# Where a scan gets its first state: from a pointer to the last one, or folded into the first column of its input

## The chip, the cores and the metric

The kernel runs on one core of one Trainium2 chip. The metric is the device time of one execution in microseconds, as the median of several runs. The profile is one execution, recorded by the hardware profiler.

## What is computed

The input x is (4, 128, 128, 128) in float32. Layer 0 is a Mamba block over each image as a sequence of 16384 positions; layer 1 is a spectral layer (Fourier transforms, a filter mix, a residual). What matters here is the recurrence of layer 0, with 256 inner channels and 16 states per channel:

```python
A = -jnp.exp(A_log)
def step(h, inp):
    d_t, B_t, C_t, u_t = inp
    dA = jnp.exp(d_t[:, :, None] * A)
    h = h * dA + d_t[:, :, None] * B_t[:, None, :] * u_t[:, :, None]
    y = jnp.einsum('bds,bs->bd', h, C_t)
    return (h, y)
```

Before it come four matrix products, a convolution of four taps, a softplus (delta) and a SiLU (u); behind it the gate, the output product and the norms.

## The kernel before

**Tiling.** A chunk is 512 positions of one image; there are 32 chunks per image and 128 in all, k from 0 to 127. The 256 channels are two halves (j). A tile has 128 partitions, which are 32 channels by 4 of the 16 states. A half needs 16 such tiles per chunk. They are worked in units of four, so a chunk has 8 units (two halves by four rounds r) of four places (p = 0 to 3), and a unit is two pairs of places. One pair is one slot: slots 0, 2, 4, ... of a chunk hold places 0 and 1 of a unit, slots 1, 3, 5, ... hold places 2 and 3. `place(r, p)` rotates which of the four channel groups m a place holds.

**One place of a unit.** ACT computes da = exp(delta * A), 512 wide (`exps`, L400), into PSUM for places 1 to 3 and into SBUF for place 0. The product du*B is `b`: for places 1 to 3 POOL multiplies tiles in SBUF into `hb` (`dbu`, L370), for place 0 PE builds it in PSUM by a transpose (`dbu_turn`, L390). DVE scans along the 512 positions (L419), the state being state * da + b. The scan takes its first state from `st`, a column with the last state of the same place in the chunk before; where a chunk opens an image, the first state is the constant 0. Then h is multiplied by C into `hb`: on DVE (L421) where `by_vector` says so, which is places 2 and 3 with a few exceptions, else on POOL (L426), where places 0 and 1 are mostly one instruction of 1024. ACT copies the last state into `st` (L422, L427). PE sums over states and channels (`sums`, L440), with `gate` (L450) behind it.

**Where the large tiles come from.** rdu and rdelta hold du and delta of one half, repeated over the states. ACT makes delta in slot 6 (`dt_act`), POOL makes du (`du_pool`, L319) in slot 7, SP stores both to DRAM (dd), and SP loads them back four times over, a load for each 32 partitions (`rep_load`, L327): for j = 0 in slot 9, for j = 1 in slot 16. The slots here are those of the chunk before: what chunk k needs at its first slot is made while chunk k-1 is scanned. rB and rC come the same way.

**The order.** It is written out by hand. Each step is put into a slot and a phase, and `manual_schedule` issues slot after slot, in each slot phase after phase:

```python
for phase in ("turn", "sums", "pe", "exps", "late", "act", "pool", "dbu", "early", "gate", "scans", "dve", "end"):
    for f in todo[n, phase]:
        f()
```

Each engine has one queue, which runs in this order. POOL's is dbu(u+1), product(u), dbu(u+2), product(u+1), and so on, with `du_pool` once a chunk. A dbu is one instruction of 1536 elements for rounds 0 and 1 and two (512 and 1024) for rounds 2 and 3, since `place` wraps round there.

**Buffers.** hb has four, h three, rdu and rdelta two each, da one in PSUM for each of places 1 to 3. The small tiles of the pool `tiny` have two. `spectrum`, which transforms some channels of layer 1 early, beside the scans, has its own tiles fx, fs and fq.

Of the kernel before, what the change touches and what calls it, by code (L numbers as in the profile page):

```python
# [26 lines left out]
F32 = mybir.dt.float32  # L27
AF = mybir.ActivationFunctionType
ALU = mybir.AluOpType
# [4 lines left out]
P = 128  # L34
T = 512
# [11 lines left out]
def kernel(ctx: ExitStack, tc: tile.TileContext, a: dict, out: bass.AP):  # L47
# [106 lines left out]
    spec = [dpool.tile([H, C, 2, WF], F32, tag=f"spec_{b}", name=f"spec_{b}") for b in range(EARLY)]  # L154
    shared = SimpleNamespace(**{k: v for k, v in locals().items() if k not in ("ctx", "tc")})
    block0(tc, shared)
    block1(tc, shared)


def block0(tc, s):  # L160
    nc, B, NCH, NH, NS, NG, ND, R, NX, KC, HALO, C, L, NF, DI = (
        s.nc, s.B, s.NCH, s.NH, s.NS, s.NG, s.ND, s.R, s.NX, s.KC, s.HALO, s.C, s.L, s.NF, s.DI,
    )
    NT, TH, HP = T // P, T // 2, P // 2
    with ExitStack() as ctx:
        def pool(name, bufs, **kw):
            return ctx.enter_context(tc.tile_pool(name=name, bufs=bufs, **kw))

        p1 = pool("p1", 1)
        p2 = pool("p2", 2)  # L170
        hpool = pool("hb", 4)
        tiny = pool("tiny", 2)
# [13 lines left out]
        st = {}  # L186
        stats, outs = s.stats, s.outs

        def pre(k):
# [3 lines left out]
            b, i = divmod(k, NCH)  # L193
            d = st[k] = {}
# [127 lines left out]
            def rep_load(j):  # L322
# [9 lines left out]
                (NP - 2, "pe", z_mm), (NP - 1, "act", z_act), (NP + 2, "act", z_silu), (3, "pe", xd_mm), (4, "act", xd_act), (5, "pe", dt_mm), (5, "pe", xd_turn),  # L332
                (5 if k else 7, "act", bc_load), (6, "act", dt_act), (7, "act", xd_turn_act), (7, "pool", du_pool),
                (8, "pe", partial(du_turn, 0)), (9, "act", partial(rep_load, 0)),
                (8, "pool", partial(bt_act, 0, 0, 1)), (9, "act", partial(bt_act, 0, 1, 5)),
                (10, "act", partial(bt_act, 0, 5, 8)), (11, "pe", partial(du_turn, 1)),
                (11, "pool", partial(bt_act, 1, 0, 1)), (12, "act", partial(bt_act, 1, 1, 2)),
# [7 lines left out]
        def norming(k):  # L345

            return k >= NCH and 2 <= k % NCH < 2 + NCH // 2

        def place(r, p):


            return (p - r) % ND

        def by_vector(k, j, r, p):

            if norming(k):
                return p > 1 and (k % 2 == 1 or (j, r, p) != (1, 2, 2))
            return p > 1 or (k % 2 == 1 and (j, r, p) == (1, 2, 1))

        def dbu(u):  # L360

            k, r = divmod(u, NH * NG)
            j, r = divmod(r, NG)
            d = st[k]
            hb = d["hb", j, r] = hpool.tile([P, ND, T], F32, tag="hb", name=f"hb_{k}_{j}_{r}")
            p = 1
            while p < NG:
                m = place(r, p)
                n = min(NG - p, ND - m)
                nc.gpsimd.tensor_tensor(  # L370
                    hb[:, p : p + n, :], d["du", j][:, m : m + n, :], d["B"][:, p - 1 : p - 1 + n, :], ALU.mult
                )
                p += n

        def pair(n):

            k, r = divmod(n, NP)
            u, p = divmod(r, ND // 2)
            j, r = divmod(u, NG)
            return k, j, r, 2 * p  # L380

        def dbu_turn(n):

            k, j, r, p = pair(n)
            d = st[k]
            if p == 0:
                b = d["b0"] = psd.tile([P, T], F32, tag="b0", name=f"b0_{k}_{j}_{r}")
                for t in range(NT):
                    src = d["bt"][:, t, j * ND + place(r, 0), :, :].rearrange("p s d -> p (s d)")
                    nc.tensor.transpose(b[:, t * P : (t + 1) * P], src, s.ident)  # L390

        def exps(n, qs):

            k, j, r, p = pair(n)
            d = st[k]
            for q in qs:
                m = place(r, p + q)
                c = (j * NG + p + q) * ND + m
                da = (psd if p + q else p2).tile([P, T], F32, tag=f"da{p + q}", name=f"da{p + q}_{k}_{j}_{r}")
                nc.scalar.activation(da, d["delta", j][:, m, :], AF.Exp, scale=s.amat[:, c : c + 1])  # L400
                d["da", j, r, p + q] = da

        def scans(n):


            k, j, r, p = pair(n)
            d = st[k]
            hb = d["hb", j, r]
            das = [d.pop(("da", j, r, p + q)) for q in range(2)]
            dve = [q for q in range(2) if by_vector(k, j, r, p + q)]  # L410
            pool = [q for q in range(2) if q not in dve]
            last = d["last", j, r, p] = tiny.tile([P, 2], F32, tag=f"st{j}_{r}_{p}", name=f"st_{k}_{j}_{r}_{p}")
            if pool:
                h = p2.tile([P, 2, T], F32, tag="h", name=f"h_{k}_{j}_{r}_{p}", bufs=3)
            for q in range(2):
                b = hb[:, p + q, :] if p + q else d.pop("b0")
                init = 0.0 if k % NCH == 0 else st[k - 1]["last", j, r, p][:, q : q + 1]
                o = das[q] if q in dve else h[:, q, :]
                nc.vector.tensor_tensor_scan(o, das[q], b, init, ALU.mult, ALU.add)  # L419
            for q in dve:  # L420
                nc.vector.tensor_tensor(hb[:, p + q, :], das[q], d["C"][:, p + q, :], ALU.mult)  # L421
                nc.scalar.copy(last[:, q : q + 1], das[q][:, T - 1 : T])  # L422
            if pool:
                q = slice(pool[0], pool[-1] + 1)
                ps = slice(p + pool[0], p + pool[-1] + 1)
                nc.gpsimd.tensor_tensor(hb[:, ps, :], h[:, q, :], d["C"][:, ps, :], ALU.mult)  # L426
                todo[n + 1, "late"].append(partial(nc.scalar.copy, last[:, q], h[:, q, T - 1]))  # L427

        def sums(u):

# [44 lines left out]
        def spectrum(b, c0, n):  # L475

            g = {}

            def load():
                g["x"] = p1.tile([s.H, 3, s.W], F32, tag="fx", name=f"fx_{b}_{c0}")  # L480
                nc.sync.dma_start(out=g["x"][:, 0:n], in_=s.x1[b][c0 : c0 + n].rearrange("c h w -> h c w"))

            def over_h():
                g["pa"] = psp.tile([s.W, 3, 2 * s.WF], F32, tag="pp", name=f"pp_fa_{b}_{c0}")
                for q in range(n):
                    nc.tensor.matmul(g["pa"][:, q], g["x"][:, q], s.fh, start=True, stop=True)

            def evict():
                g["sa"] = p1.tile([s.W, 3, 2 * s.WF], F32, tag="fs", name=f"fs_{b}_{c0}")
                nc.scalar.copy(g["sa"][:, 0:n], g["pa"][:, 0:n])  # L490

            def over_w():
                half = s.H // 2
                g["px"] = psp.tile([s.H, 3, 2 * s.WF], F32, tag="pp", name=f"pp_fx_{b}_{c0}")
                for q in range(n):
                    re, im = g["sa"][:, q, 0 : s.WF], g["sa"][:, q, s.WF :]
                    for (data, a, b_), start in (((re, s.fwr, s.fwr), True), ((im, s.fwi, s.fwm), False)):
                        for at, w in ((0, a), (1, b_)):
                            o = g["px"][at * half : (at + 1) * half, q]
                            nc.tensor.matmul(o, data[:, at : at + half], w, start=start, stop=not start)  # L500

            def store():
                x = p1.tile([s.H, 3, 2, s.WF], F32, tag="fq", name=f"fq_{b}_{c0}")
                nc.scalar.copy(x[:, 0:n].rearrange("h c r k -> h c (r k)"), g["px"][:, 0:n])  # L504
                nc.sync.dma_start(out=s.spec[b][:, c0 : c0 + n], in_=x[:, 0:n])

            return [
                (4, "pe", load), (12, "pe", over_h), (12, "end", evict), (13, "pe", over_w), (13, "end", store),
            ]

        n_chunks = B * NCH
        todo = defaultdict(list)
# [33 lines left out]
        for n in range(n_chunks * NP):  # L546
            if n % 2 == 0:
                todo[n - 3, "early"].append(partial(exps, n, (0,)))
            todo[n - 1, "exps"].append(partial(exps, n, (1,) if n % 2 == 0 else (0, 1)))
            todo[n - 1, "turn"].append(partial(dbu_turn, n))  # L550
            todo[n, "scans"].append(partial(scans, n))
            if n % 2 == 0:
                todo[n - 2, "dbu"].append(partial(dbu, n // 2))
            else:
                todo[n + 2, "sums"].append(partial(sums, n // 2))
        slots = [n for n, _ in todo]
        with tc.manual_schedule():
            for n in range(min(slots), max(slots) + 1):
                for phase in ("turn", "sums", "pe", "exps", "late", "act", "pool", "dbu", "early", "gate", "scans", "dve", "end"):
                    for f in todo[n, phase]:  # L560
                        f()

# [509 lines left out]
```

## Time and profile before

| what | value |
|---|---|
| median of 3 runs | 7097.85 us (7094.02 to 7100.94) |
| profiled execution, its own time | 7100.83 us |
| its span, first to last instruction | 7099.1 us |
| busy DVE, POOL, ACT, PE | 96%, 96%, 87%, 80% of the span |
| scans, L419 | 4096 instructions, 60 to 6384 us |
| of these from the constant 0 | 128 |
| last stage (layer 1) | 6384 us to the end |

Busy shares are of the whole span, and the two stages have different limits. A line of a group tells its line in the code, the engine, the operation and its tiles (out<-in), then how often it ran, its busy time in us and the mean of one in ns, and behind the last bar the time that the engine stood idle before it and what ended that. Consecutive DVE instructions overlap by some tens of ns, so the sum of means is above the busy time; the distance of starts is what one costs. A DMA's row tells its issue; its landing is told apart.

### The profile page before, as it was taken

What the parts mean: (1) busy time and instruction counts of PE and PEld (TensorE: products, weight loads), DVE (VectorE), ACT (ScalarE), POOL (GpSimd) and SP (SyncE); (2) the same over time, 40 slices, a digit from 0 to 9 for tenths busy, and PEclk for the clock granted to TensorE, in tenths of its full rate; (3) what the DMA queues carried; (4) which work ended last, traced back from release to release, by engine and by line L of the source; (5) the groups of instructions that cost most, each with busy time, mean ns of one, the idle gap of its engine ahead of it and who ended that gap; (6) DMA issues with size and microseconds to landing.
All of it is one profiled execution on the core that took longest, in us unless ns stands there. A gap on an engine that the chain in (4) does not pass through costs nothing.

```text
span 7099.1 us, 95554 instructions
## 1 busy us (share of the span) xinstructions
PE 5656.9 (80%) x28724; PEld 2700.3 (38%) x28724; DVE 6843.7 (96%) x7901; ACT 6144.4 (87%) x13836; POOL 6807.6 (96%) x3010
## 2 busy tenths in 40 slices
PE   6777777787777778787787778887778787877999
PEld 2333333333333333333333333333333333327888
DVE  6999999999999999999999999999999999997877
ACT  6888888888888888888989888898988989878886
POOL 6999999999999999999999999999999999997887
PEclk8988898888989989999999999999999999989999
DMA  6667667667787767777777777777878777768865
GB/s 141 160 153 164 159 149 165 160 150 175 179 196 181 188 169 167 181 181 179 192 193 196 189 174 177 174 184 172 200 188 200 191 170 178 169 143 293 273 218 190
DMA packets 759513, 1288.54 MB, mean 182 GB/s; under 512 B 81728, under 2 KB 192848, under 8 KB 758992
## 3 DMA queue, kind: packets, MB, share of 16 engines
q1 hardware_dynamic: 758848, 1282.16, 72.5%
q8 instruction: 226, 3.70, 0.2%
q14 instruction: 295, 2.42, 0.1%
q10 hardware_dynamic: 144, 0.26, 0.0%
HBM read 1025.52 MB, written 256.58 MB: 181 GB/s over the span
## 4 chain that ended last, share of the span: by engine, by line
ACT 30%; DVE 24%; POOL 18%; PE 10%; issue 10%; DMA 7%; SPq 1%; DVEq 0%; ACTq 0%; POOLq 0%
DVE da L419 12%; ACT da L400 12%; POOL hb L370 10%; POOL hb L426 7%; DVE h L419 7%; ACT L400 3%; DVE hb L421 3%; DMA rdelta<-dd 2%; ACT bt L313 2%; PE px L892 2%; DMA rdu<-dd 2%; ACT L247 2%; ACT L283 1%; ACT delta L283 1%; PE y L440 1%
## 5 line engine op out<-in xcount | busy, mean ns | idle before, releaser
L370 POOL TENSOR_TENSOR hb<-rdu,rB 128x1536 f32<-128x1536 f32 (+2 forms) x1536 | 3612.4, 2370 | 41.6 <-DMA rdelta<-dd 21.2
L400 ACT ACTIVATE da<-rdelta,amat 128x512 f32<-128x512 f32 x4096 | 2792.3, 699 | 123.3 <-DVE h L419 119.3
L426 POOL TENSOR_TENSOR hb<-h,rC 128x1024 f32<-128x1024 f32 (+1 forms) x1048 | 2411.1, 2302 | 89.3 <-DVE h L419 76.6
L419 DVE TENSOR_TENSOR_SCAN da<-da,st,hb 128x512 f32<-128x512 f32 x2000 | 2449.3, 1268 | 38.0 <-ACT da L400 27.1
L421 DVE TENSOR_TENSOR hb<-da,rC 128x512 f32<-128x512 f32 x2064 | 1309.7, 673 | 2.2
L419 DVE TENSOR_TENSOR_SCAN h<-da,st,b 128x512 f32<-128x512 f32 x992 | 1258.7, 1269 | 1.9 <-PE b L390 1.9
L440 PE MATMUL y<-hb,sel 128*32 128x512 f32 x8192 | 1243.4, 681 | 2.9 <-POOL hb L426 2.7
L419 DVE TENSOR_TENSOR_SCAN h<-da,st,hb 128x512 f32<-128x512 f32 x976 | 1223.1, 1255 | 1.4 <-ACT da L400 1.4
L390 PE MATMUL b<-ident,bt 128*128 128x128 f32 x4096 | 723.7, 298 | 448.9 <-DVE h L419 325.2
L239 PE MATMUL pp_cv<-xm,wck 128*128 128x512 f32 x2048 | 1013.7, 640 | 1.5 <-ACT xm L222 0.8
L313 ACT ACTIVATE bt<-pt_dut,xdt 128x256 f32<-128x256 f32 x2048 | 837.6, 473 | 181.1 <-PE pt_dut L302 180.9
L390 PEld LDWEIGHTS b<-ident,bt 128*128 128x128 f32 x4096 | 524.6, 151 | 943.2 <-DVE h L419 650.7
L422 ACT COPY st<-da 128x1 f32<-128x1 f32 x2064 | 267.9, 160 | 441.3 <-DVE hb L421 437.0
L239 PEld LDWEIGHTS pp_cv<-xm,wck 128*128 128x128 f32 x2048 | 396.0, 204 | 651.7 <-issue 420.8
L302 PE MATMUL pt_dut<-ident,du 128*128 128x128 f32 x1024 | 207.8, 337 | 407.2 <-POOL du L319 391.4
L850 POOL TENSOR_TENSOR wb<-wb,term 128x1040 f32<-128x1040 f32 x166 | 398.8, 2403 | 62.0 <-ACT term L840 56.6
L436 PE MATMUL y<-u,diag 128*128 128x512 f32 x512 | 303.3, 676 | 183.7 <-DVE zs L450 181.8
L277 PE MATMUL pp_dt<-xd,wdt 128*128 128x256 f32 x1024 | 299.2, 418 | 149.9 <-ACT pp_o L464 141.2
L302 PEld LDWEIGHTS pt_dut<-ident,du 128*128 128x128 f32 x1024 | 132.2, 165 | 652.6 <-POOL du L319 528.5
L400 ACT ACT_TABLE_LOAD x262 | 336.1, 1283 | 12.2 <-DMA rdelta<-dd 7.6
L319 POOL TENSOR_TENSOR du<-delta,u 128x1024 f32<-128x1024 f32 x128 | 301.1, 2353 | 29.4 <-ACT delta L283 27.9
L228 PE MATMUL pp_z<-xm,win 128*128 128x512 f32 x512 | 275.6, 636 | 59.5 <-ACT fq L504 53.7
(167 smaller groups left out, 8209.6 us busy)
## 6 DMA issues: line engine op xcount, KB each, us to landing
rdelta<-dd SPq DMA_DIRECT2D x1024, 256.0 KB, 4.8
rdu<-dd SPq DMA_DIRECT2D x1024, 256.0 KB, 7.8
rC<-bc SPq DMA_DIRECT2D x512, 256.0 KB, 7.4
rB<-bc SPq DMA_DIRECT2D x512, 192.0 KB, 4.6
dd<-delta SPq DMA_DIRECT2D x256, 256.0 KB, 7.7
dd<-du SPq DMA_DIRECT2D x128, 512.0 KB, 6.6
ft<-in_filt_w SPq DMA_DIRECT2D x108, 520.0 KB, 6.7
ob<-o SPq DMA_DIRECT2D x128, 256.0 KB, 2.1
```

What stands on the lines that cost most here:

```text
L239: nc.tensor.matmul(ps["cv", j], w, d["xm"][:, t : t + T], start=t == 0, stop=t == KC - 1)
L302: nc.tensor.transpose(ps["dut"][:, 2 * t + j, :], d["du"][:, j, at : at + P], s.ident)
L313: nc.scalar.activation(d["bt"][:, 2 * h + t, :, q, :], src, AF.Copy, scale=d["xdt"][:, 2 * h + t, R + q : R + q + 1])
L370: nc.gpsimd.tensor_tensor(hb[:, p : p + n, :], d["du", j][:, m : m + n, :], d["B"][:, p - 1 : p - 1 + n, :], ALU.mult)
L390: nc.tensor.transpose(b[:, t * P : (t + 1) * P], src, s.ident)
L400: nc.scalar.activation(da, d["delta", j][:, m, :], AF.Exp, scale=s.amat[:, c : c + 1])
L419: nc.vector.tensor_tensor_scan(o, das[q], b, init, ALU.mult, ALU.add)
L421: nc.vector.tensor_tensor(hb[:, p + q, :], das[q], d["C"][:, p + q, :], ALU.mult)
L426: nc.gpsimd.tensor_tensor(hb[:, ps, :], h[:, q, :], d["C"][:, ps, :], ALU.mult)
L436: nc.tensor.matmul(y, s.diag[:, j, :], d["u"][:, j, :], start=True, stop=False)
L440: nc.tensor.matmul(y[m * DG : (m + 1) * DG, :], s.sel, d["hb", j, r][:, p, :], start=False, stop=r == NG - 1)
L850: nc.gpsimd.tensor_tensor(wb, wb, u[n].terms[f], ALU.add)
```

## The change

The scans of places 1 to 3 start from the constant 0 in every chunk. What the first state would have added at the first position, da[0] * last state, is added to the first column of b instead, so the states are the same. For this:

- POOL's dbu writes columns 1 to 511 of `hb` alone.
- `first_products` (DVE): for one half, the first column of du*B for all three places and four channel groups, 12 elements per partition, read from column 0 of rdu and rB; and, unless the chunk opens an image, the exponents delta[0] * A, 16 elements, from column 0 of rdelta. `first_exp` (ACT) takes the exponential, `first_mult` (DVE) multiplies by the last states, `first_add` (DVE) adds both, twice over, into a tile of 24 (a copy where the chunk opens an image).
- `first` (ACT), once per unit, in a new phase ahead of "early": a copy of three of these elements into column 0 of places 1 to 3 of `hb`.
- The last states of a half become one tile of 16 columns; the order of the places in it lets one product take them all. Place 0 still reads its first state from there.
- `by_vector` gives DVE the product of place 1 in (j, r) = (1, 2) in all chunks without `norming`, where it was every second; and in chunks with it, POOL's exception (1, 2, 2) goes.
- `spectrum` works in one tile instead of three.

```diff
+                (12, "dve", partial(first_products, k, 0)), (13, "late", partial(first_exp, k, 0)),
+                (14, "gate", partial(first_mult, k, 0)), (14, "dve", partial(first_add, k, 0)),
+                (20, "dve", partial(first_products, k, 1)), (21, "late", partial(first_exp, k, 1)),
+                (21, "dve", partial(first_mult, k, 1)), (22, "gate", partial(first_add, k, 1)),
...
             if norming(k):
-                return p > 1 and (k % 2 == 1 or (j, r, p) != (1, 2, 2))
-            return p > 1 or (k % 2 == 1 and (j, r, p) == (1, 2, 1))
+                return p > 1
+            return p > 1 or (j, r, p) == (1, 2, 1)
...
-                    hb[:, p : p + n, :], d["du", j][:, m : m + n, :], d["B"][:, p - 1 : p - 1 + n, :], ALU.mult
+                    hb[:, p : p + n, 1:],
+                    d["du", j][:, m : m + n, 1:],
+                    d["B"][:, p - 1 : p - 1 + n, 1:],
+                    ALU.mult,
...
+        def first_products(k, j):
+            d = st[k]
+            du = d["du", j][:, :, 0:1].rearrange("p m o -> p o m")
+            b = d["B"][:, :, 0:1]
+            f = d["f", j] = tiny.tile([P, NG - 1, 1, ND], F32, tag=f"f{j}", name=f"f_{k}_{j}")
+            shape = [P, NG - 1, ND]
+            nc.vector.tensor_tensor(f[:, :, 0, :], du.to_broadcast(shape), b.to_broadcast(shape), ALU.mult)
+            if k % NCH:
+                e = d["e", j] = tiny.tile([P, NG, ND], F32, tag=f"e{j}", name=f"e_{k}_{j}")
+                a = s.amat.rearrange("p (j g m) -> p j g m", j=NH, m=ND)[:, j]
+                now = d["delta", j][:, :, 0:1].rearrange("p m o -> p o m")
+                nc.vector.tensor_tensor(e, a, now.to_broadcast([P, NG, ND]), ALU.mult)
+
+        def first_exp(k, j):
+            if k % NCH:
+                nc.scalar.activation(st[k]["e", j], st[k]["e", j], AF.Exp)
+
+        def first_mult(k, j):
+            if k % NCH:
+                e = st[k]["e", j]
+                nc.vector.tensor_tensor(e, e, st[k - 1]["last", j], ALU.mult)
+
+        def first_add(k, j):
+            shape = [P, NG - 1, 2, ND]
+            f = st[k]["f2", j] = tiny.tile(shape, F32, tag=f"g{j}", name=f"g_{k}_{j}")
+            b = st[k]["f", j].to_broadcast(shape)
+            if k % NCH:
+                e = st[k]["e", j][:, 1:].rearrange("p g (c m) -> p g c m", c=1)
+                nc.vector.tensor_tensor(f, b, e.to_broadcast(shape), ALU.add)
+            else:
+                nc.vector.tensor_copy(f, b)
+
+        def first(u):
+            k, r = divmod(u, NH * NG)
+            j, r = divmod(r, NG)
+            at, step = ND - r + 1, 2 * ND + 1
+            f = st[k]["f2", j].rearrange("p g c m -> p (g c m)")
+            nc.scalar.copy(st[k]["hb", j, r][:, 1:NG, 0], f[:, at : at + 2 * step + 1 : step])
...
-                init = 0.0 if k % NCH == 0 else st[k - 1]["last", j, r, p][:, q : q + 1]
+                m = place(r, 0)
+                init = 0.0 if p + q or k % NCH == 0 else st[k - 1]["last", j][:, 0, m : m + 1]
...
-                g["x"] = p1.tile([s.H, 3, s.W], F32, tag="fx", name=f"fx_{b}_{c0}")
+                g["f"] = p1.tile([s.H, 3, 2 * s.WF], F32, tag="fx", name=f"fx_{b}_{c0}")
...
                 todo[n - 2, "dbu"].append(partial(dbu, n // 2))
+                todo[n - 1, "first"].append(partial(first, n // 2))
```

More of the change, by code (lines that the diff above doesn't have):

```diff
@@ L411, in scans @@
             pool = [q for q in range(2) if q not in dve]
-            last = d["last", j, r, p] = tiny.tile([P, 2], F32, tag=f"st{j}_{r}_{p}", name=f"st_{k}_{j}_{r}_{p}")
+            if (j, r, p) == (j, 0, 0):
+                d["last", j] = tiny.tile([P, NG, ND], F32, tag=f"st{j}", name=f"st_{k}_{j}")
+            last = d["last", j].rearrange("p g m -> p (g m)")
+            at = [(p + q) * ND + place(r, p + q) for q in range(2)]
             if pool:
@@ L421, in scans @@
                 nc.vector.tensor_tensor(hb[:, p + q, :], das[q], d["C"][:, p + q, :], ALU.mult)
-                nc.scalar.copy(last[:, q : q + 1], das[q][:, T - 1 : T])
+                nc.scalar.copy(last[:, at[q] : at[q] + 1], das[q][:, T - 1 : T])
             if pool:
@@ L426, in scans @@
                 nc.gpsimd.tensor_tensor(hb[:, ps, :], h[:, q, :], d["C"][:, ps, :], ALU.mult)
-                todo[n + 1, "late"].append(partial(nc.scalar.copy, last[:, q], h[:, q, T - 1]))
+                a, b = at[pool[0]], at[pool[-1]]
+                to = last[:, a : b + 1 : max(b - a, 1)]
+                todo[n + 1, "late"].append(partial(nc.scalar.copy, to, h[:, q, T - 1]))
         def sums(u):
@@ L479, in load @@
             def load():
-                g["x"] = p1.tile([s.H, 3, s.W], F32, tag="fx", name=f"fx_{b}_{c0}")
-                nc.sync.dma_start(out=g["x"][:, 0:n], in_=s.x1[b][c0 : c0 + n].rearrange("c h w -> h c w"))
+                g["f"] = p1.tile([s.H, 3, 2 * s.WF], F32, tag="fx", name=f"fx_{b}_{c0}")
+                nc.sync.dma_start(out=g["f"][:, 0:n, 0 : s.W], in_=s.x1[b][c0 : c0 + n].rearrange("c h w -> h c w"))
             def over_h():
@@ L485, in over_h @@
                 for q in range(n):
-                    nc.tensor.matmul(g["pa"][:, q], g["x"][:, q], s.fh, start=True, stop=True)
+                    nc.tensor.matmul(g["pa"][:, q], g["f"][:, q, 0 : s.W], s.fh, start=True, stop=True)
             def evict():
-                g["sa"] = p1.tile([s.W, 3, 2 * s.WF], F32, tag="fs", name=f"fs_{b}_{c0}")
-                nc.scalar.copy(g["sa"][:, 0:n], g["pa"][:, 0:n])
+                nc.scalar.copy(g["f"][:, 0:n], g["pa"][:, 0:n])
             def over_w():
@@ L495, in over_w @@
                 for q in range(n):
-                    re, im = g["sa"][:, q, 0 : s.WF], g["sa"][:, q, s.WF :]
+                    re, im = g["f"][:, q, 0 : s.WF], g["f"][:, q, s.WF :]
                     for (data, a, b_), start in (((re, s.fwr, s.fwr), True), ((im, s.fwi, s.fwm), False)):
@@ L502, in store @@
             def store():
-                x = p1.tile([s.H, 3, 2, s.WF], F32, tag="fq", name=f"fq_{b}_{c0}")
-                nc.scalar.copy(x[:, 0:n].rearrange("h c r k -> h c (r k)"), g["px"][:, 0:n])
+                nc.scalar.copy(g["f"][:, 0:n], g["px"][:, 0:n])
+                x = g["f"].rearrange("h c (r k) -> h c r k", r=2)
                 nc.sync.dma_start(out=s.spec[b][:, c0 : c0 + n], in_=x[:, 0:n])
@@ L558, in block0 @@
             for n in range(min(slots), max(slots) + 1):
-                for phase in ("turn", "sums", "pe", "exps", "late", "act", "pool", "dbu", "early", "gate", "scans", "dve", "end"):
+                for phase in ("turn", "sums", "pe", "exps", "late", "act", "pool", "dbu", "first", "early", "gate", "scans", "dve", "end"):
                     for f in todo[n, phase]:
```

## The prediction

> **What bounds the kernel now.** I read busy time by engine, then the stages, then the groups by form, then the timeline of one chunk. In a middle stage (columns: PE, PEld, DVE, ACT, POOL busy):
>
> ```profile
> DVE  6999999999999999999999999999999999997877
> POOL 6999999999999999999999999999999999997887
> 3300.00:4840.00 1540.00, 1227.57 (x5834) 534.63 (x5834) 1525.84 (x1627) 1381.44 (x3149) 1515.56 (x662) 0.94 0.76 184
> ```
>
> DVE works 99% of these 1540 us, POOL 98%, ACT 90%. The scans (60 to 6384 us) are one stage in which DVE and POOL are both full: a microsecond gained on one alone is lost to the other soon, and a microsecond in which DVE stands still is not made good. What a first state costs stands in the groups by form (count | busy, mean ns), since the first chunk of each of the 4 images already starts from 0:
>
> ```profile
> L419 DVE TENSOR_TENSOR_SCAN da<-da,st,hb 128x512 f32<-128x512 f32 x2000 | 2449.3, 1268 | 38.0 <-ACT da L400 27.1 <-POOL hb L370 8.9 <-issue 1.2
> L419 DVE TENSOR_TENSOR_SCAN h<-da,st,hb 128x512 f32<-128x512 f32 x976 | 1223.1, 1255 | 1.4 <-ACT da L400 1.4
> L419 DVE TENSOR_TENSOR_SCAN da<-da,hb 128x512 f32<-128x512 f32 x64 | 74.5, 1210 | 1.1 <-issue 0.9
> L419 DVE TENSOR_TENSOR_SCAN h<-da,hb 128x512 f32<-128x512 f32 x32 | 38.3, 1197 | 3.9 <-POOL hb L370 3.7 <-ACT da L400 0.2
> ```
>
> So a constant saves 58 ns. Starts agree: a unit (4 scans, 2 products) takes 5.89 us in the timeline (1019.46 to 1025.35) and 5.65 us in the first chunk (59.91 to 65.56).
>
> Two things in the timeline decide. First, how DVE fares beside POOL when it has small operands in SBUF:
>
> ```profile
> 90.05 3.44 POOL L370 TENSOR_TENSOR hb<-rdu,rB 128x1536 f32<-128x1536 f32 x1
> 90.92 2.65 DVE L138 TENSOR_SCALAR weff<-wagg,gn_gamma 128x128 f32<-128x128 f32 x1
> 93.44 2.36 POOL L426 TENSOR_TENSOR hb<-h,rC 128x1024 f32<-128x1024 f32 x1
> 93.61 2.34 DVE L139 SCALAR_TENSOR_TENSOR weff<-wagg,gn_gamma,weff 128x128 f32<-128x128 f32 x1
> 95.87 0.15 DVE L144 TENSOR_TENSOR bias<-pp_bias,agg_b 128x1 f32<-128x1 f32 x1
> ```
>
> L138 ends 0.08 us after POOL's product, L139 at 95.95 when the next ends (95.80); L129, the like of L138 with POOL idle, took 0.23 us. L144 has one input in PSUM and doesn't wait. Nor does any scan, product or gate: each has one input in PSUM. Second, when rdu of the next chunk lands:
>
> ```profile
> 1018.64 2.35 POOL L319 TENSOR_TENSOR du<-delta,u 128x1024 f32<-128x1024 f32 x1
> ...
> 1021.01 0.37 SPq L320 DMA_DIRECT2D dd<-du  x1
> ...
> 1027.39 1.74 SPq L327 DMA_DIRECT2D rdu<-dd  x4
> ...
> 1033.04 1.26 DVE L419 TENSOR_TENSOR_SCAN da<-da,st,hb 128x512 f32<-128x512 f32 x1
> ...
> 1034.33 0.69 DVE L421 TENSOR_TENSOR hb<-da,rC 128x512 f32<-128x512 f32 x1
> ...
> 1037.32 3.42 POOL L370 TENSOR_TENSOR hb<-rdu,rB 128x1536 f32<-128x1536 f32 x1
> DMA to landing us min/median/max: 5.4/7.8/10.5
> ```
>
> The scan at 1033.04 is the second of slot 12, L421 its product; DVE leaves the slot at 1034.94. The last rdu load (from 1028.69) lands 7.8 us later, at 1036.46. Over the 46 chunks whose four landings the trace tells, the last landing is 1.3 to 6.0 us, 3.1 in the mean, after the end of that scan. POOL's first product of rdu starts 3.9 us after it (median), so today almost nobody waits.
>
> **What the Trainium skill says.** SBUF — State Buffer, section "Who interferes with whom": a DVE instruction with two SBUF inputs, or in a two-port mode, and a GpSimd instruction reading SBUF exclude each other for the whole instruction; the later one blocks. L138, L139 and L144 agree. Perfetto Trace Analysis, section "Optimizing Scalar/DVE Operations": some 60 ns fixed for DVE on SBUF; the 512-element product starts the next after 0.59 us, which agrees.
>
> **The change, part by part.** Gains and small prices on DVE:
> - 3 scans in 4, 124 chunks of 128: 2976 x 0.058 = 173 us off.
> - by_vector moves a 512 product from POOL to DVE in 40 even chunks without norm and 24 with: 64 x 0.59 = 38 us on. POOL loses 40 x (2.37 - 1.29) + 24 x 1.29 = 74 us.
> - Small instructions: first_products 256 + 248, first_mult 248, first_add 256 = 1008, estimated at 0.08 us of pitch (60 ns and 12 to 24 elements): 81 us.
> Sum -54 us, -0.4 per chunk.
>
> New stalls of DVE, per chunk:
> - **first_products of j=0, behind slot 12, needs rdu.** It comes a product (0.6) later than the scan's end; DVE is 3 x 0.17 = 0.5 us faster over the three units since du, and POOL's du some 0.25 earlier (the product before it starts 0.33 us after slot 6's scans now, at once when POOL waits for them). Wait: 3.1 - 0.6 + 0.5 - 0.25 = 2.75 us. Behind it on DVE's queue stand the second product, slot 13's scans and products; for those wait ACT (first_exp, copies, exps), POOL's next product, PE. Below: 0.95 (smallest landing); above: 5.65.
> - **The port there.** POOL's own next product (1536, 3.4 us) waits for the same landing. Either it gets in before the first small product or between the two, and DVE waits 3.4; or both small ones slip through: 0. I take 3.4, as L138/L139 show POOL getting in between.
> - first_mult in slot 14 finds POOL idle (its next product needs slot 14's scans): 0. first_add behind those scans: 0, as DVE's queue goes on before POOL hears.
> - **The port at j=1.** Behind slot 4 POOL is just done with its dbu (median rest 0.05 us). If the pair of small products passes, POOL runs its product (2.3) and the dbu of unit 4 (3.4) until 5.75 after slot 4; first_mult, behind slot 5 (3.4 later), waits some 2.3, and first_add follows free. If it doesn't pass, the second waits 2.3 there and first_mult is free. 2.3 either way, up to 3.5.
> Sum 2.75 + 3.4 + 2.3 = 8.45; with -0.4, 8.05 us per chunk, x 127 = 1022 us.
>
> Elsewhere, at no cost:
> - ACT gets 1024 `first` copies of 3 elements (0.19, like st<-h) and 248 exps (0.2 to 0.3): some 255 us, 2.0 per chunk; copies of last states +40. It idles some 5 us per chunk in that stage. A scan of place 1 now waits for `first`, which stands behind slot n-1's ACT work: ACT has 4.7 us from the release of da1 to that scan, the exp and copy take 0.9, and `first` is late only where that slot holds over 3.5 us. Stalls give it more room. Without that cover: up to 2 us in one or two units of a chunk.
> - `first` and POOL's dbu write different columns of hb; were they ordered, ACT would wait for a dbu that is done within 2 us of that point.
> - POOL's 511-wide rows: no view shows them. Rows of 65 in the last stage (L917) cost 1394 ns for 520 elements, where the 512 row takes 1283: under 15 ns a row. Bounds -0 to +10% of dbu's 28 us, which POOL then has room for.
> - Spectrum's three tiles become one: the next load waits for a store seven slots (20 us) earlier that lands in 1.9. SP's queue gets no new DMA.
> - `last` as one tile: ACT's copies write other columns; readers come a chunk later.
> - The last stage (6384 to the end) is untouched.
>
> The profiled execution took 7100.83 us around a span of 7099.1, 3 us above the median of 7097.85. 7097.85 + 1022 is about 8120.
>
> **The rivals.**
> - *Port harmless for tiny operands, landing not*: 2.75 - 0.4 = 2.35 per chunk, 298 us: 7395. For it: no small product of two SBUF tensors runs beside POOL today, and 12 elements might pass. Against: L139.
> - *Every small instruction blocked*: three waits for a whole POOL product (2.4) and five for the rest of one (1.3, half the length-weighted mean of POOL's instructions) make 13.7; with POOL busy 0.8 of the time, 11; with the landing 13.35 per chunk, 1695 us: 8793. For it: POOL is full today. Against: it idles once DVE stalls.
> - *Faster*: the landing comes before slot 12 ends and the port isn't contended; then -54 on DVE, -74 on POOL: 7045. It decides if rdu lands 3 us sooner; only an earlier du on POOL would do that. Against: not one of the 46 landings is early enough.
> - That scans don't take a constant is excluded by the code and the 128 that already do.
>
> **How the numbers follow.** Main case 0.5 (7850 to 8400), port harmless 0.2 (7300 to 7500), more blocking 0.22, faster 0.04, other small losses 0.04, of which 0.01 no change. A change under 0.2% couldn't be told from none here. Range 7390 to 8600.
>
> **What would show it.** Right: scans of places 1 to 3 near 1200 ns; DVE idle at the first small product of j=0, ended by a DMA of rdu, some 350 us in all; small products with means of 0.5 us and more, their maximum about 3.4; POOL busy below 90% in this stage and idle before L426's line for DVE; ACT below 90%. Wrong: small products at 0.15 us throughout, no wait for rdu, or a chunk period below 49 us.

## The result, and the profile after

The changed kernel takes 7899.61 us (median of 4 runs, 7887.12 to 7914.8) against 7098.72 us before: a ratio of 1.1131, with a 95% interval of 1.1117 to 1.1145. It is 801 us slower. Its profiled execution spans 7885.3 us, 786 more than the profile before.

The stage that stood at 99% for DVE and 98% for POOL, in the third image of the changed kernel (same columns: PE, PEld, DVE, ACT, POOL busy; at the end the granted TensorE clock, the share of the DMA engines and GB/s):

```profile
3660.00:5400.00 1740.00, 1301.53 (x5779) 558.58 (x5782) 1674.05 (x1869) 1405.03 (x3425) 1485.56 (x647) 0.85 0.67 161
```

A chunk of the last three images takes 56.3 us where it took 49.5; one of the first image takes 53.2 where it took 48.8. DVE is still busy for 96% of the stage, but POOL only for 85%, and ACT for 81%. The granted TensorE clock is lower than before, 0.85 instead of 0.94, but that isn't what costs the time: DVE stands idle for PE for under 3 us in all the scans together. "Busy" has to be read with care here. The prediction's "port" is the way to SBUF that a DVE instruction with two SBUF inputs and POOL can only have one at a time, and an instruction that stands and waits for it counts as busy. The groups by form show it (count | busy, mean ns | idle before, releaser):

```profile
L475 DVE TENSOR_TENSOR_SCAN da<-da,hb 128x512 f32<-128x512 f32 x2128 | 2481.4, 1208 | 10.6 <-ACT hb L442 7.4 <-ACT da L452 1.9 <-issue 0.3
...
L421 DVE TENSOR_TENSOR e<-e,st 128x16 f32<-128x16 f32 x248 | 323.3, 1304 | 0.8 <-ACT e L416 0.8
L412 DVE TENSOR_TENSOR e<-amat,rdelta 128x16 f32<-128x16 f32 x248 | 300.1, 1210 | 0.2
...
L407 DVE TENSOR_TENSOR f<-rdu,rB 128x12 f32<-128x12 f32 x256 | 142.2, 555 | 227.2 <-DMA rdu<-dd 99.5 <-DMA xr<-in_x 62.4 <-DMA rdelta<-dd 40.2
...
L431 DVE TENSOR_TENSOR g<-f,e 128x24 f32<-128x24 f32 x248 | 41.5, 167 | 4.2
```

The scans are at 1208 ns, as the constant promised. But products of 16 elements take as long as scans of 512, in the mean. Of the 227 us of idle time ahead of L407, 40 belong to the first chunk of all. The other 187 are the wait for rdu, though the profile puts 72 of them down to DMAs of x, which L407 does not read: all of them go when L407 no longer reads the rdu that has just been loaded (below, "No landing to wait for"). And POOL, that was full, now waits for DVE (its products with C; they read h, so they wait for the scans, even where the profile names the small instruction that ended last):

```profile
L482 POOL TENSOR_TENSOR hb<-h,rC 128x1024 f32<-128x1024 f32 x944 | 2230.1, 2362 | 966.7 <-DVE g L431 421.6 <-DVE h L475 368.3 <-DVE f L407 92.5
```

The timeline of one chunk has both places. For j = 0, behind slot 12:

```profile
1172.80 3.59 POOL L374 TENSOR_TENSOR hb<-rdu,rB 128x1022 f32<-128x1022 f32 x2
...
1174.30 0.69 DVE L477 TENSOR_TENSOR hb<-da,rC 128x512 f32<-128x512 f32 x1
1175.62 0.80 DVE L407 TENSOR_TENSOR f<-rdu,rB 128x12 f32<-128x12 f32 x1 [0.62 <-DMA rdu<-dd]
1176.35 1.31 DVE L412 TENSOR_TENSOR e<-amat,rdelta 128x16 f32<-128x16 f32 x1
1176.36 1.26 POOL L482 TENSOR_TENSOR hb<-h,rC 128x512 f32<-128x512 f32 x1
```

DVE stands idle for 0.62 us until rdu lands. Then L407 starts at 1175.62 and ends at 1176.42, with POOL's running product (1176.39); L412 ends at 1177.66, with POOL's next (1177.62). For j = 1, behind slots 4 and 5:

```profile
1148.05 0.14 DVE L407 TENSOR_TENSOR f<-rdu,rB 128x12 f32<-128x12 f32 x1
1148.11 0.17 DVE L412 TENSOR_TENSOR e<-amat,rdelta 128x16 f32<-128x16 f32 x1
1148.20 2.37 POOL L482 TENSOR_TENSOR hb<-h,rC 128x1024 f32<-128x1024 f32 x1 [0.24 <-DVE f L407]
...
1150.51 3.45 POOL L374 TENSOR_TENSOR hb<-rdu,rB 128x1533 f32<-128x1533 f32 x1
1151.64 2.36 DVE L421 TENSOR_TENSOR e<-e,st 128x16 f32<-128x16 f32 x1
1154.03 0.18 DVE L431 TENSOR_TENSOR g<-f,e 128x24 f32<-128x24 f32 x1
```

The first two pass before POOL starts; L421 arrives 1.13 us into POOL's product and ends with it (1153.96), and L431 is free again. It is so in the whole trace: the 360 small products that took over 0.3 us all end 0.02 to 0.05 us behind an instruction of POOL, and none of the 640 others lies inside one. The trace's records split by half and line give the bill per chunk (means; own duration about 0.16):

| DVE | j = 0 | j = 1 |
|---|---|---|
| idle ahead of L407, for a DMA | 1.47 | 0 |
| L407, f | 0.96 | 0.15 |
| L412, exponents | 2.25 | 0.17 |
| L421, first_mult | 0.29 | 2.32 |
| L431, first_add | 0.15 | 0.18 |

The stalls are 1.47 + 0.81 + 2.09 + 0.14 + 2.17 = 6.7 us per chunk, 837 us over the chunks that have them. The means hide a spread: the idle time ahead of L407 is 2.72 us where the chunk that is being scanned has `norming` work too (48 of them), 0.94 in the 47 others of the last three images and 0.38 in the first image.

### The profile page after: what moved, and what is told of

It is laid out like the page before. It is cut to its first block, busy times and chain, and to the rows that moved or that the text cites. A ratio compares the mean times of both kernels' runs of the same rounds, so it can differ in the third digit from the quotient of the medians.

```text
span 7885.3 us, 98596 instructions
## 1 busy us (share of the span) xinstructions
PE 5926.0 (75%) x28724; PEld 2785.8 (35%) x28724; DVE 7459.9 (95%) x8973; ACT 6309.2 (80%) x15148; POOL 6740.8 (85%) x2986
## 5 line engine op out<-in xcount | busy, mean ns | idle before, releaser
L374 POOL TENSOR_TENSOR hb<-rdu,rB 128x1533 f32<-128x1533 f32 (+2 forms) x1536 | 3599.1, 2359 | 21.9 <-DMA rdelta<-dd 21.1
L482 POOL TENSOR_TENSOR hb<-h,rC 128x1024 f32<-128x1024 f32 (+1 forms) x1024 | 2332.0, 2277 | 966.7 <-DVE g L431 421.6
L475 DVE TENSOR_TENSOR_SCAN da<-da,hb 128x512 f32<-128x512 f32 x2128 | 2481.4, 1208 | 10.6 <-ACT hb L442 7.4
L397 PE MATMUL b<-ident,bt 128*128 128x128 f32 x4096 | 782.8, 320 | 793.0 <-DVE h L475 755.0
L498 PE MATMUL y<-hb,sel 128*32 128x512 f32 x8192 | 1369.5, 746 | 2.7 <-POOL hb L482 2.6
L475 DVE TENSOR_TENSOR_SCAN h<-da,hb 128x512 f32<-128x512 f32 x944 | 1127.9, 1195 | 14.3 <-ACT hb L442 9.4
L397 PEld LDWEIGHTS b<-ident,bt 128*128 128x128 f32 x4096 | 572.1, 163 | 1314.5 <-DVE h L475 1053.0
L228 PE MATMUL pp_z<-xm,win 128*128 128x512 f32 x512 | 335.1, 757 | 422.6 <-ACT fx L560 408.4
L416 ACT ACTIVATE e<-e 128x16 f32<-128x16 f32 x248 | 51.8, 209 | 407.9 <-DVE e L412 407.5
L407 DVE TENSOR_TENSOR f<-rdu,rB 128x12 f32<-128x12 f32 x256 | 142.2, 555 | 227.2 <-DMA rdu<-dd 99.5
L452 ACT ACT_TABLE_LOAD x262 | 336.1, 1283 | 12.3 <-DMA rdelta<-dd 7.7
```

Source lines behind the costliest of these rows:

```text
L228: nc.tensor.matmul(ps["z", j], w, d["xm"][:, HALO:], start=True, stop=True)
L374: nc.gpsimd.tensor_tensor(hb[:, p : p + n, 1:], d["du", j][:, m : m + n, 1:], d["B"][:, p - 1 : p - 1 + n, 1:], ALU.mult,)
L498: nc.tensor.matmul(y[m * DG : (m + 1) * DG, :], s.sel, d["hb", j, r][:, p, :], start=False, stop=r == NG - 1)
```

## The experiments

All are compared with the kernel before (7095 to 7097 us in these runs).

**The constant alone.** How much is the gain worth when nothing pays for it? This kernel leaves out the small products and the copies of first columns, and with them the carry of the states of places 1 to 3.

```diff
-                (12, "dve", partial(first_products, k, 0)), (13, "late", partial(first_exp, k, 0)),
...
-                todo[n - 1, "first"].append(partial(first, n // 2))
...
-                    hb[:, p : p + n, 1:],
+                    hb[:, p : p + n, :],
```

> Leaves out the carry of states from chunk to chunk for places 1 to 3: scans from the constant 0 and by_vector as changed, no small products, dbu over all 512 columns. Theory (the port and the landing cost the time, the constant pays 58 ns a scan): 2976 x 0.058 = 173 us off and 38 us of moved products on, with POOL relieved by 74 us, so about 6965 us, 130 below before, and no DVE instruction over 1.3 us. Rival (POOL is the real bound, so that DVE's gain is lost): 7025 us or more, 74 below at best, with DVE waiting for POOL.

Measured: 6983.74 us, ratio 0.9838 (0.9824 to 0.9853). 113 us of the 135 expected come through, so the gain on DVE is real, and the rival is out. Both engines are full again, DVE 1520.50 and POOL 1522.45 of 1540 us in the window of the third image. Over all the scans DVE's busy time fell by 128 us, from 6274 to 6146, nearly what was expected, but its idle time rose by 15: its waits for ACT's exps rise from 29 us to 47, and those for POOL's dbu fall from 13 to 4.

**The same products on POOL.**

```diff
-            nc.vector.tensor_tensor(f[:, :, 0, :], du.to_broadcast(shape), b.to_broadcast(shape), ALU.mult)
+            nc.gpsimd.tensor_tensor(f[:, :, 0, :], du.to_broadcast(shape), b.to_broadcast(shape), ALU.mult)
```

and likewise for the other four lines.

> The changed kernel, with first_products, first_mult and first_add on POOL instead of DVE; ACT's parts and all slots stay. Theory (port): no DVE instruction has two SBUF inputs any more, so all of DVE's small stalls go, 800 us with the wait for rdu; POOL pays 8 instructions of 0.2 to 0.3 us, some 2 us per chunk, and waits for rdu where its dbu waits anyway: 7050 to 7200 us. Rival (small products are slow by themselves, through broadcast or column reads or through the chain exp, product, sum): POOL or ACT carries the time instead, and it stays over 7500.

Measured: 7338.98 us, ratio 1.0343 (1.0327 to 1.0358). This is 561 us below the changed kernel, but 140 above the expected range. On POOL the small instructions take 0.21 to 0.23 us each, whatever half and line, so they are not slow by themselves. What is left is a new wait, in the list of waits of this kernel (us in total, times, longest):

```profile
ACT e L416 <- POOL e L412: 397.3, 194, 4.8
...
DVE h L475 <- ACT hb L442: 243.6, 233, 4.3
```

POOL comes to the exponents late (in the chunk at 1221 us 1.44 us of that is rdu's landing), ACT stands at first_exp until then, and DVE's next scan waits for the `first` copy behind it on ACT's queue.

**The disputed cost by itself.** Two kernels that are the one before plus a small product behind slots 5 and 13, with both inputs in SBUF:

```diff
+            if n % 8 == 5:
+                probe = tiny.tile([P, 16], F32, tag="probe", name=f"probe_{n}")
+                nc.vector.tensor_tensor(probe, s.amat[:, 16:32], s.amat[:, 0:16], ALU.mult)
```

> The kernel before, plus one product of 16 by 16 elements on DVE behind slots 5 and 13 of each chunk (256 in all), both inputs constants in SBUF, the result unused. Theory (port): each stands until POOL's running instruction ends, behind slot 5 about 2.3 us, behind slot 13 1 to 2.5; means near 2 us, and 300 to 550 us more, POOL making good a part. Rival (own cost): 0.15 us each, 20 to 25 us more.

or with one of them in PSUM (`das[1][:, 0:16]` in place of `s.amat[:, 16:32]`):

> As the run with two SBUF inputs, but one of the two inputs is 16 columns of place 3's da in PSUM. Theory (port): no wait, 0.15 us each, 256 x 0.08 = 20 us more: 7110 to 7135. Rival (any small DVE instruction at these places waits, for whatever reason): as slow as the run with two SBUF inputs.

The line of the added product, first with two inputs in SBUF, then with one in PSUM (count: duration in ns, min/median/max):

```profile
L425 DVE TENSOR_TENSOR probe<-amat x256: 164/2396/5555, 82.1 to 6839.7; 128x16 f32<-128x16 f32 x128
```

```profile
L425 DVE TENSOR_TENSOR probe<-da,amat x256: 174/174/176, 84.3 to 6499.5; 128x16 f32<-128x16 f32 x128
...
  ACT st L422: 119.4, 256
```

With two inputs in SBUF: 7555.96 us, ratio 1.0648 (1.0631 to 1.0666). The product takes 2.40 us behind slot 5 and 1.58 behind slot 13, 468 us above its own 0.16; the time rose by 459. It waits in 253 of 256 places, and each time it ends 0.03 us behind an instruction of POOL. With one in PSUM: 174 to 176 ns in every one of 256 places, though in 201 of them one instruction of POOL runs from before it to after it. So the wait belongs to the second SBUF input and not to the place, the size or the chain. The second kernel still missed its time: 7216.08 us, ratio 1.0167 (1.0152 to 1.0183), 120 us instead of 20. The last line above says why: DVE idles 119.4 us ahead of the added product, for ACT's copy of the last state out of the same da tile, behind which the product was ordered: it starts 0.03 us after that copy each time. That was a flaw of the experiment and not a wait for the port. Why two reads of one tile were put in order no run shows.

**One slot later for j = 0**, so that rdu has landed:

```diff
-                (12, "dve", partial(first_products, k, 0)), (13, "late", partial(first_exp, k, 0)),
-                (14, "gate", partial(first_mult, k, 0)), (14, "dve", partial(first_add, k, 0)),
+                (13, "dve", partial(first_products, k, 0)), (14, "late", partial(first_exp, k, 0)),
+                (14, "dve", partial(first_mult, k, 0)), (14, "end", partial(first_add, k, 0)),
```

> The changed kernel, with the chain of j = 0 one slot later: first_products behind slot 13, first_exp and first_mult in slot 14, first_add behind first_mult; rdu has landed by then. Theory (port): the wait for rdu (1.47 us per chunk in the changed kernel) goes, but first_products now meets POOL's product of 1533 for the next chunk and waits some 2 us for its rest, and first_add, behind slot 14's scans, finds POOL's next product started and waits 2.3: 4.3 per chunk where it was 4.5 with the landing, so 7850 to 7900. Rival (the landing is a stall of its own beside a fixed price of the small products): 187 us less, 7710.

Measured: 7992.81 us, ratio 1.1264 (1.1248 to 1.1279): slower than the change by 93 us, and outside both expectations. The groups by form of this kernel:

```profile
L431 DVE TENSOR_TENSOR g<-f,e 128x24 f32<-128x24 f32 x248 | 322.2, 1299 | 8.4
...
L407 DVE TENSOR_TENSOR f<-rdu,rB 128x12 f32<-128x12 f32 x256 | 308.5, 1205 | 42.6 <-DMA rdelta<-dd 41.3 <-issue 0.6 <-DMA rdu<-dd 0.3
L412 DVE TENSOR_TENSOR e<-amat,rdelta 128x16 f32<-128x16 f32 x248 | 157.8, 636 | 0.0
```

No wait for rdu is left. For j = 0, L407 takes 2.26 us and L431, which was free, 2.42, as the theory had it; L412 takes 1.10 in the mean, since in 28% of the chunks POOL's next product still gets in between. That is 5.3 us of stalls instead of 4.5, times 127 about 105 us; 93 were measured. The wait did not vanish with its cause; the port took it over, and more.

**No landing to wait for.** The first columns of j = 0 are read from the other half's tiles of the chunk before:

```diff
-            du = d["du", j][:, :, 0:1].rearrange("p m o -> p o m")
+            own = (d, j) if j or k == 0 else (st[k - 1], 1)
+            du = own[0]["du", own[1]][:, :, 0:1].rearrange("p m o -> p o m")
...
-                now = d["delta", j][:, :, 0:1].rearrange("p m o -> p o m")
+                now = own[0]["delta", own[1]][:, :, 0:1].rearrange("p m o -> p o m")
```

> The changed kernel, with the first columns of j = 0 read from the other half's rdu and rdelta of the chunk before, which have long landed (so they are not the right values); all else as changed. Theory (port and landing add up, but POOL's phase moves): no wait for a DMA; first product 0.7 us, exponents 1.3 (one half of POOL's split dbu or the short product), and first_mult in slot 14 now meets POOL's 1533 product for 0.7: 2.7 per chunk instead of 4.5, some 7670 us. Rival A (the landing alone goes, nothing else moves): 187 us less, 7710. Rival B (the port takes all of it back): 7880 to 7900.

Measured: 7686.75 us, ratio 1.0831 (1.0816 to 1.0846), 213 below the changed kernel. The groups by form (first_mult, exponents, first product; this kernel's lines are one further down, and both halves are in each):

```profile
L422 DVE TENSOR_TENSOR e<-e,st 128x16 f32<-128x16 f32 x248 | 469.5, 1893 | 0.8 <-ACT e L417 0.8
L413 DVE TENSOR_TENSOR e<-amat,rdelta 128x16 f32<-128x16 f32 x248 | 183.5, 740 | 0.0
...
L408 DVE TENSOR_TENSOR f<-rdu,rB 128x12 f32<-128x12 f32 x256 | 115.5, 451 | 42.6 <-DMA rdelta<-dd 42.6
```

No wait for a DMA is left but the first chunk's. For j = 0 the products take 0.75 and 1.31 us, as expected, but first_mult 1.47 instead of 0.7. So of 1.47 us idle and 3.0 of port per chunk the idle time went, and the port took 3.1 where 2.7 were expected. Rival B is out. Between the theory and rival A the time can't decide, 17 us from the one and 23 from the other: the pieces of the port's bill did move, as the theory has it, but its sum stayed, as rival A has it.

**On POOL, at the right places.** The exponents are split off and everything is put ahead of POOL's large products:

```diff
+                (12, "pool", partial(first_exponents, k, 0)), (13, "late", partial(first_exp, k, 0)),
+                (14, "pool", partial(first_mult, k, 0)), (14, "pool", partial(first_products, k, 0)),
+                (14, "pool", partial(first_add, k, 0)),
```

and the same at 20, 21 and 22 for j = 1.

> Small products on POOL as before, but put where POOL has the data and ahead of its large products: exponents behind slot 12's and 20's start, first_mult, first_products and first_add ahead of the dbu of slots 14 and 22. Theory (the 240 us over before in the first run on POOL are DVE's waits for `first`, which ACT reaches late because it stands behind first_exp, which waits for a POOL that lags): those waits go, DVE and POOL are both full again, POOL with 1.75 us more per chunk than with the constant alone: 7080 to 7150. Rival (POOL's small instructions cost more than their 0.22 us, or ACT has no room): over 7250.

Then with one product more per chunk on DVE:

```diff
-                return p > 1
-            return p > 1 or (j, r, p) == (1, 2, 1)
+                return p > 1 or (j, r, p) == (0, 2, 1)
+            return p > 1 or (j, r, p) in ((1, 2, 1), (0, 2, 1))
```

> As e6_pool_early, with one product of C more per chunk moved from POOL to DVE, place 1 of unit (0, 2): POOL 1.08 us less, DVE 0.59 more per chunk, which makes both about equal at 48.6 to 49.3 us per chunk against 49.5 before: 7030 to 7080, a little faster than before. Rival (ACT, 95% full with the copies of first columns, is the bound now): 7100 or more, and no faster than e6_pool_early.

and then with the `first` phase ahead of "act":

```diff
-                for phase in ("turn", "sums", "pe", "exps", "late", "act", "pool", "dbu", "first", "early", "gate", "scans", "dve", "end"):
+                for phase in ("turn", "sums", "pe", "exps", "late", "first", "act", "pool", "dbu", "early", "gate", "scans", "dve", "end"):
```

> e7_pool_shift, with the phase of ACT's `first` copies ahead of ACT's other work of a slot instead of behind it. There DVE waited 48 us for these copies in all. If DVE's queue is still what sets the end, up to 48 us go: 7040 to 7070. Rival (POOL, 98% busy, takes the place of the wait, or ACT, now standing at the copy until POOL's sum is there, delays the exps): 7080 to 7110, no faster than e7_pool_shift.

Measured: 7148.85 us (ratio 1.0075, 1.0062 to 1.0089), 7084.67 (0.9983, 0.9976 to 0.999) and 7073.13 (0.9969, 0.9957 to 0.9981). The first is at the upper edge of its range, the second 5 us above its own, and the third 3 us above its own, but below what its rival said. The third is 22 us faster than the kernel before and the fastest that computes all. In the first, POOL is the fuller engine, 1525.93 of 1540 us against DVE's 1485.52; in the second they are level, 1512.47 for POOL and 1519.91 for DVE. DVE's waits for the copies fall with the last step (the list of waits, second kernel, then third):

```profile
DVE h L480 <- ACT hb L447: 33.9, 59, 2.0
...
DVE da L480 <- ACT hb L447: 14.6, 27, 1.1
```

```profile
DVE da L480 <- ACT da L457: 33.1, 65, 3.0
DVE h L480 <- ACT hb L447: 17.1, 51, 1.2
```

Of 48 us 17 are left, but DVE's waits for the exps rise from 9 to 33: those now stand behind the copies on ACT's queue. So 12 us came and not 31.

## Why the prediction was right, and where it was off

Direction, causes and places held; 8120 us was 220 too high, inside the range.

- **Gain.** 173 - 38 = 135 us was forecast for the constant with the moved products; the constant alone brought 113. Small products were put at 81 us of their own, 0.08 each, and the trace agrees: one that isn't blocked starts the next after 0.07 to 0.10 us (medians). The 0.59 us of the 512-element product was no test of the 60 ns for SBUF, since its input da lies in PSUM; L407, with both inputs in SBUF, starts the next after 0.067. So without stalls -32 instead of -54; with the 837 us of stalls that makes 805. 801 were measured, and 786 between the two profiled executions, so the bill closes to within 20 us.
- **The landing** is the term that was mis-sized: 2.75 us forecast, 1.47 measured. Its other pieces were near: over the same 46 chunks POOL's du starts 0.2 us earlier behind slot 6 (0.25 forecast), and DVE needs 0.7 less for the three units (0.5 forecast). But the step took the chain from du to landing as it was, and it became 1.8 us shorter: the store of du lands after 4.8 us instead of 6.6, so the last rdu lands 14.8 us behind du's end instead of 16.6. The next point has where this comes from.
- **Why the landing came sooner.** In each of the eleven kernels the store of du lands 1.4 to 1.6 us (mean) behind the store of delta that was issued before it, as if it stood in line behind it. Where it is issued 2.4 to 3.1 us after that one, it lands in 6.0 to 6.9 us; where 4.4 to 4.9 us after, in 4.4 to 4.8. The store of delta comes from ACT and doesn't move with DVE's stall (5.9 us behind slot 5's scans before, 6.2 after). But du stands behind slot 6's scans, and these behind the stall of first_mult: it ends 10.6 us behind slot 5's scans instead of 8.5. The kernel before with two SBUF inputs in the added product has that stall (and one behind slot 13), nothing else changed, and the same short store, 4.5 us in the mean. Read so, the port's wait at j = 1 itself took most of the 1.8 us off the landing: the sum held as independent two terms that aren't. No run varied the two stores alone, so that they stand in line is a reading of these runs.
- **The port at j = 0.** 3.4 forecast; 2.9 measured (0.81 + 2.09). The picture was right that POOL gets in between the two: L412 waits in 120 of 124 chunks. Wrong was that POOL's next product is the large one and waits for the same landing: POOL waits 0.5 us for rdu in all, since its queue holds a running dbu and slot 12's product ahead of it. So L407 pays the rest of what runs, and L412 what comes next: the 1533 product in 53 chunks (3.45 us), the short product of 512 in 44, the 511 part of a dbu in 16, a product of 1024 in 7. Where DVE had stood idle for over 2 us, it was the 1533 one in 41 of 44 chunks; where under 1 us, in none of 52. So the earlier landing made this term smaller too, as far as these counts tell.
- **The port at j = 1.** 2.3 forecast for first_mult, with the pair before it and the sum behind it free: 2.17, 0.01, 0.02. The two inputs in SBUF of L139 were the key; the Trainium skill's SBUF — State Buffer, "Who interferes with whom", has it that issue order decides who blocks, and here L407 and L412 pass, and L421 doesn't, for their order with POOL alone: L421 starts 1.13 us after POOL's product in the timeline above, the other two before it.
- **Forecast as free**: first_mult of j = 0 mostly was (0.14, blocked in 13% of the chunks), first_add was (0.15 in every chunk), ACT's copies were (17 us of DVE's idle time in all), POOL's rows of 511 were (3437 ns instead of 3454).
- **The rivals.** "Port harmless for tiny operands" falls with 16 elements that wait 2.40 us. "Every small instruction blocked" falls with j = 1's first two at 0.15 and 0.17. "Faster" fell with the landing, which was more than 0.3 us late in 98 of 127 chunks; in the other 29 it was in time or nearly so, which none of the 46 landings before would have been.
- Of the forecast signs, the idle time for rdu was 187 us instead of 350; the others came as written (largest exponents product 3.478 us, POOL 85%, ACT 81%), but for first_add, which stayed at 0.17 us and had been forecast as free.

## What to carry to other kernels

Before a small DVE instruction is put beside a busy POOL, look where its inputs are: in these runs two tensors in SBUF made it wait for whatever product POOL was running, one in PSUM didn't, and 12 elements waited as 128 do. A profile books that wait as busy time, so compare the duration of a small instruction with the same form elsewhere before believing a 96%. And work that moves earlier in a hand-written order has to be held against the landing of its data, instruction by instruction; moving it later instead can hand the wait to the next shared thing. And the terms of such a sum need not be independent: a stall in one place moves what is issued behind it, and here it seems to have shortened the next wait.

## What was not expected of the hardware

- POOL's products of 12 to 24 elements take 0.21 to 0.23 us in the mean, with broadcast and column reads (0.28 at most); on DVE the same take 0.14 to 0.18 unblocked. The small ones are nearly equal, where at 512 elements POOL takes 1275 ns and DVE 673. POOL's large ones say it already: the line through its 511 and 1533 products (1275 and 3437 ns) is 0.19 us plus 2.1 ns per element, an estimate of 0.22 to 0.24 for these.
- Rows of 511 floats that start one float late cost POOL nothing: 3437, 2364 and 1275 ns against 3454, 2371 and 1283 for the full ones.
- The store of du landed after 4.8 us instead of 6.6 with nothing changed in it. It was issued 1.9 us later behind the store of delta, and in both kernels it landed 1.5 us behind that one.
